# Moving the small convolution between two output products, and stores and scalings to other places, in a fused state-space scan kernel

## The chip, the core and the metric

The kernel runs on one core of a Trainium2 chip. The core has a matrix engine (TensorE, PE), a vector engine (VectorE, DVE), a scalar engine (ScalarE, ACT), a general engine (GpSimd, POOL) and a queue engine (SyncE, SP), from which nearly all transfers of this kernel are issued. The metric is the device time of one execution in microseconds.

## The reference

The input x is (4, 128, 96, 96) in float32. It is normalised in 32 groups of channels. Each image is then read as a sequence of 9216 positions in four directions: by rows forwards and backwards, by columns forwards and backwards. All four go through the same block, and its outputs are fused by a 1x1 convolution and added to x:

```python
t = grouped1x1(x, in_proj)            # 128 -> 512 channels, 4 groups
u, gate = t[:, :256], t[:, 256:]
u = depthwise_conv5(silu(u))
s = ssm_in @ u                        # 32 channels
a = clip(0.999 + 0.0009 * sigmoid(ssm_delta @ u + b), 0.0001, 0.9999)
bb, cc = tanh(ssm_b @ u + b), tanh(ssm_c @ u + b)
h = scan(h * a + bb * s)              # along the sequence (written with cumsums)
u = u + ssm_out @ (cc * h + d * s)
y = out_proj @ (grouped1x1(u * sigmoid(gate), mix))
```

## The kernel before, in words

Two directions are done together: as two streams s = 0 and 1, one forwards and one backwards. A *phase* is one image in one order (columns, V, or rows, H); there are eight. A phase has six *steps* of 1536 positions, a step four *pairs* of units (p = 0 to 3, one unit for each stream). A unit has 384 columns, every fourth position of the step. The main loop calls `pair(t)` for t = 0 to 191; k is t modulo 4. The work of several stages is overlapped by hand: in pair t

- the *front* (`front`, `compute_front`) computes silu of the input projection for pair t+4,
- the *convolution* and the *projections* (`taps`, `conv`, `conv_less`, `proj`) are done for pair t,
- the *scan* (`scan`) runs over half of the step before, when k is 0 or 1,
- `outputs` multiplies the state for pair t-5,
- the gates, `out_of` and `gating` finish pair t-6, whose product with the fused weights, W (`accumulate`), comes one pair later still.

The instruction order of every engine is the program's order, written out by hand.

Because the two streams run over one image from its two ends, in the second half of a phase they meet data that the first half has computed: silu is then loaded from a copy in DRAM (`keep_silu`, `load_silu`), and the gates too (`kept`, `load_kept`). So there are kinds of pairs. Counted by t modulo 24: in pairs 8 to 17 gates are computed and no front ("gates alone"); in 18 and 19 neither; in 20 to 23 and 0 to 5 a front, with gates loaded from DRAM (called `old`); in 6 and 7 both front and gates. The flag `ahead` is true in all but the first six pairs and pairs 6 and 7.

The 256 channels of u come in two halves. Half 0 is convolved on TensorE: `conv` (weights `band`, 128 rows by 32 columns of the array) and `conv_less` (weights `less`, 64 rows by 32 columns) add into two PSUM banks, and a copy for each stream brings the sum to `us[i]`. Half 1 is convolved by five taps: the first on ScalarE (`first_tap`, L609), four on VectorE (L611), with the running sum in PSUM banks 0 and 1. The same banks take the output products afterwards: `under` (L501) copies u there as the start of the sum, and `out_of` (L493) adds the matmuls of the state; the gating (L563) multiplies by the gate. Banks 4 to 7 are shared by W, convolution, gates and projections; in pairs without a front the convolution has banks 7 and 6, the two W have 4 and then 5, the projections 4 and 5, and the four gates the banks of `GATE[False]`.

In a gates-alone pair TensorE's order is: `conv`, W, W, `conv_less`, then four `gate` and four `out_of` matmuls (32 rows by 128 columns), then the projections. ScalarE's order is: first `under`, copy of W (L714 or L712), second `under`, copy of W, copies of u (L594; in pairs with k of 2 and 3 the second of them is VectorE's), four gate tanhs (L509), first tap, scaling of s (L664), and the three evacuations of the projections (L639 to L641). VectorE also takes bn_stats (L397) of the next image's chunks, in V phases with k of 2 and 3; the chunks are loaded by `load_chunks` (L393).

Of the kernel before, what the change touches and what calls it, by code (L numbers as in the profile page):

```python
# [55 lines left out]
R = 4  # L56
LN = 16
NS = HH // LN
N = LN * WW // R
# [7 lines left out]
def conv_preact_kernel(  # L67
# [51 lines left out]
    psum = ps.tile([P, 8, 512], F32, name="psum")  # L119
    SSM, TAPS, PROJ = 0, 0, (4, 5)  # L120
    FRONT = (7, 6, 2, 3)
    GATE = {True: (6, 4, 5, 7), False: (4, 5, 7, 6)}

    def plan(with_front):

# [2 lines left out]
    def bank(i):  # L128
        return psum[:, i, :]
# [287 lines left out]
    def front_parts(i, banks):  # L417

        step, g = divmod(i, R)
        if step * UB >= NU:  # L420
            return
        st = step % NS
        if st == NS // 2:
            sils[step] = sils[step - 1]
            load_silu(step + 1, (g,))
        elif st == NS - 1 and g < 2:
            load_silu(step, (2 * g, 2 * g + 1))
        elif g == 0 and fresh(step):
# [12 lines left out]
        for s in range(2):  # L441
            load_front(step + 1, s, slice(64 * s + 32, 64 * s + 64), slice(g, g + 1))
        if g == R - 1:
            for s in range(2):
                load_front(step + 1, s, slice(64 * s, 64 * s + 32), slice(0, R))
        if step:
            keep_silu(step, g)

    def keep_silu(step, g):
        st = step % NS  # L450
        if st < NS // 2 - 1:
            nc.sync.dma_start(kept_sil[step // NS % 2][st][g], sils[step][:, :, :, g, :])

    def load_silu(step, gs):
        if 0 in gs:
# [44 lines left out]
        seeded.add(bi)  # L500
        nc.scalar.copy(psum[:, SSM + 2 * s : SSM + 2 * s + 2, :N], us[bi][:, s])  # L501

    def sigmoids(bi, banks):
        bn = stats[units[bi]["b"]][1]
        n = bi // 2
        gv = gates[n % 2]
        for s in range(2):
            for j in range(2):
                nc.scalar.activation(  # L509
                    gv[:, s, j, :],  # L510
                    bank(banks[2 * s + j])[:, :N],
                    AF.Tanh,
                    bias=bn[:, 2 + j : 3 + j],
                    scale=0.5,
                )
# [49 lines left out]
    us = {}  # L565
# [10 lines left out]
    def conv(i, banks):  # L576

        step, p = units[i]["step"], units[i]["p"]
        sil, k = blocks(step), less_of(p)
        for s in range(2):  # L580
            for g in range(4):
                mm(bank(banks[s]), g, band[:, s, p, g, :], columns(step, sil[s][:, g, :], 1 - k),
                   True, False)

    def conv_less(i, banks, copies=(nc.scalar.copy, nc.scalar.copy)):
        step, p = units[i]["step"], units[i]["p"]
        sil, k = blocks(step), less_of(p)
        for g in range(4):
            for s in range(2):
                r = less_rows(s, p)  # L590
                mm(bank(banks[s]), g, less[r, p, g, :], columns(step, sil[s][r, g, :], k),
                   False, True)
        for s, copy in enumerate(copies):
            copy(us[i][:, s, 0, :], bank(banks[s])[:, :N])  # L594

    def new_u(i):
        us[i] = wk.tile([P, 2, 2, N], F32, tag="u", bufs=LAG + 2, name=f"u_{units[i]['id']}")
# [22 lines left out]
    scans, tbs, tms = {}, {}, {}  # L620
    qb, qc, qa, qs = (slice(MH * i, MH * (i + 1)) for i in range(4))

    def proj(i, banks):

        step, p = units[i]["step"], units[i]["p"]
        if step not in scans:
            t0 = wk.tile([P, N, R], F32, tag="t0", name=f"t0_{step}")
            scans[step] = t0.rearrange("p n r -> p r n")
        ta = scans[step]
        tb = tbs[i] = wk.tile([P, N], F32, tag="t1", bufs=LAG + 1, name=f"t1_{units[i]['id']}")  # L630

        for j in (1, 0):
            for bk, cols in zip(banks, ((qb, qb, qa, qa), (qs, qs, qc, qc))):
                for c in range(4):
                    mm(bank(bk), c, w_proj[:, j, cols[c]], us[i][:, c % 2, j, :], j == 1, j == 0)
        pa, pb = (bank(bk)[:, :N] for bk in banks)

        tm = tms[i] = wk.tile([P, N], F32, tag="tm", name=f"tm_{units[i]['id']}")
        nc.scalar.activation(tm, pa, AF.Tanh, bias=b_proj[:, 0:1])  # L639
# [93 lines left out]
        return add  # L733


    later = []

    waiting = []

# [7 lines left out]
    def pair(t):  # L747
        i, k, bi = 2 * t, t % R, 2 * (t - LAG)
        back = bi >= 0
        old = back and mirror(bi // 2) is not None  # L750

        late = bi > 2 and (bi - 2) % (NU // B) == 0
        with_front = fresh((t + R) // R)
        seed = old or back and not with_front

        ahead = old or back and not with_front
        banks, w = plan(with_front or not back)
        if back:
            front(t + R, FRONT)
        if seed and not with_front:  # L760
            under(bi, 1)
        send()

        if len(reload) == 4 and (k == 1 or late):
            for b, r in reload:
                nc.sync.dma_start(accf[:, r], xr[b, :, r])
            reload.clear()
        new_u(i)
        taps(i, range(1, K))
        if t and clip_late(i - 2):  # L770
            nc.vector.tensor_scalar(*decay(i - 2)[1])
        conv(i, banks)
        if not ahead:
            conv_less(i, banks)
        if not back:
            first_tap(i + 2)
            front(t + R, FRONT)
        recurrence(t)
        un = units[i]
        stats_chunks(t)  # L780

        def stats_piece():
            if later and k > 1:
                next(later[0], None)

        if not ahead:
            free[0] = w[1]
            stats_piece()
        if seed and with_front:
            for s in (1, 0):  # L790
                under(bi, s)
        if waiting and not late:
            accumulate(waiting.pop(0), w[0])()
        if seed and not with_front:
            under(bi, 0)
        if ahead:
            accumulate(waiting.pop(0), w[1])()
            free[0] = w[0]
            stats_piece()

            other = nc.vector.tensor_copy if k > 1 and not old else nc.scalar.copy
            conv_less(i, banks, (nc.scalar.copy, other))
        if old:
            for s in range(2):
                for j in range(2):
                    out_of(bi, s, j)
                load_gate(bi + s + UB)
        elif back:
            gates_and_out(bi, with_front)
        if back:  # L810
            for s in range(2):
                gating(bi, s)
        if un["order"] == "V" and un["b"] + 1 < B and un["st"] == NS - 1 and k == R - 1:
            later[:] = [stats_finish(un["b"] + 1)]
        if t + 1 < NU // 2:
            load_chunks(t + 1)
        if back:
            load_kept(bi // 2 + 2)
            if waiting:
                add = accumulate(waiting.pop(0), w[1])  # L820
                if not late:
                    add()
            first_tap(i + 2)
            scale_s(i - 2)
        if t == NU // 2 - 1:
            for s in range(2):
                under(bi + 2, s)
        proj(i, PROJ)
        if not back and t > 0:
            scale_s(i - 2)  # L830
        if late:
            add()
            accumulate(waiting.pop(0), w[1])()
        if back:
            waiting.extend(units[bi : bi + 2])
        if t == NU // 2 - 3:
            load_last()
        if t < R:
            keep_silu(0, t)

        if bi > 0 and bi % (NU // B) == 0:
            send()

    def tail():

        first, banks = NU // 2 - LAG, (6, 7, 4, 5)

        for op in decay(NU - 2):
            nc.vector.tensor_scalar(*op)
        scale_s(NU - 2)  # L850
# [127 lines left out]
```

## Time and profile before

| | |
|---|---|
| median time of 3 runs | 1869.56 us (1867.16 to 1872.62) |
| profiled run, span | 1866.4 us, mean granted clock 0.99 |
| TensorE busy | 1827.3 us, 98% |
| ScalarE, VectorE, GpSimd busy | 1542.6, 1561.9, 1567.0 us |
| share of SP's transfers in 16 DMA engines' time | 51.5% |
| mean traffic | 172 GB/s |

The profile page gives each engine's busy time, the clock, the chain of work that ended last, and groups of instructions by line. L133 is the helper that records most matmuls: they are told apart by the tiles they read (`w_fin` for W, `main` for the projections, `sil,band` and `sil,less` for the convolution). A float32 matmul stands as two passes in the trace.

### The profile page before, as it was taken

The page shows a single profiled execution, that of the slowest core. Times are in us where ns is not written, and L with a number is a line of the kernel's source. Part 1 is how long each engine was busy: PE and PEld are TensorE (multiplying, and loading weights), DVE is VectorE, ACT ScalarE, POOL GpSimd, SP SyncE. Part 2 cuts the span into 40 slices and gives each one's busy share as a digit, 9 for nine tenths or more (in the row PEclk, how much of TensorE's full clock was granted, in tenths as well). Part 3 has the DMA queues.
Part 4 walks back from the last instruction along what each step waited for, and adds up shares of the span by engine and source line. Part 5 has one row for each costly group of instructions (what it writes and reads, how often), then busy time and mean ns, then how long its engine had stood idle before and what let it go on. Part 6 is the DMA issues. An engine that isn't in the chain of part 4 may idle for free.

```text
span 1866.4 us, 57669 instructions
## 1 busy us (share of the span) xinstructions
PE 1827.3 (98%) x24024; PEld 691.4 (37%) x24024; DVE 1561.9 (84%) x1573; ACT 1542.6 (83%) x2841; POOL 1567.0 (84%) x1615
## 2 busy tenths in 40 slices
PE   6899999999999999999999999999999999999998
PEld 3234333443334433344333433334333443334432
DVE  4698878888888988888889898888887888878886
ACT  4688888888888888888888888888888888888875
POOL 6388988888879899888887989888888889997886
PEclk7999999999999999999999999999999999999999
DMA  5564463433875557243596556433467634535424
GB/s 194 162 197 145 146 207 118 168 141 126 274 244 202 169 155 215 86 158 131 186 301 217 167 162 207 152 130 126 139 224 234 231 113 156 191 118 175 145 102 171
DMA packets 147828, 321.21 MB, mean 172 GB/s; under 512 B 14192, under 2 KB 115696, under 8 KB 147568
## 3 DMA queue, kind: packets, MB, share of 16 engines
q1 hardware_dynamic: 147136, 316.56, 51.5%
q8 instruction: 190, 3.11, 0.7%
q10 hardware_dynamic: 432, 0.96, 0.1%
q14 instruction: 70, 0.57, 0.1%
HBM read 185.21 MB, written 132.25 MB: 170 GB/s over the span
## 4 chain that ended last, share of the span: by engine, by line
PE 87%; ACT 4%; POOL 3%; DVE 2%; DMA 1%; issue 1%; SPq 0%; POOLq 0%; DVEq 0%; ACTq 0%
PE psum L133 73%; PE psum L487 7%; PE psum L493 7%; ACT sil L476 1%; DMA xs<-in_xr 1%; ACT psum L609 1%; DVE u L563 1%; DVE psum L611 1%; POOL acc L728 1%; POOL t L644 1%; ACT u L594 0%; POOL t L647 0%; DMA x_in<-in_xs 0%; POOL t L687 0%; POOL t L688 0%
## 5 line engine op out<-in xcount | busy, mean ns | idle before, releaser
L611 DVE SCALAR_TENSOR_TENSOR psum<-sil,small,psum 128x768 f32<-128x768 f32 x576 | 589.0, 1023 | 39.1 <-ACT psum L609 13.5
L133 PE MATMUL psum<-u,w_fin 128*32 128x384 f32 x6144 | 535.6, 488 | 0.0
L133 PE MATMUL psum<-u,main 128*32 128x384 f32 x6144 | 534.9, 489 | 0.3 <-DVE u L611 0.3
L563 DVE SCALAR_TENSOR_TENSOR u<-gate,psum 128x768 f32<-128x768 f32 x376 | 349.9, 952 | 165.9 <-ACT u L594 91.6
L728 POOL TENSOR_TENSOR acc<-ys,acc 128x384 f32<-128x384 f32 x376 | 412.7, 1118 | 21.6 <-ACT ys L714 4.3
L687 POOL TENSOR_TENSOR t<-t,t 64x384 f32<-64x384 f32 x192 | 263.8, 1374 | 78.0 <-DVE t L681 58.0
L133 PEld LDWEIGHTS psum<-u,w_fin 128*32 128x32 f32 x6144 | 195.9, 110 | 303.3 <-issue 223.6
L501 ACT COPY psum<-u 128x768 f32<-128x768 f32 x352 | 277.6, 802 | 34.9 <-DVE u L611 28.8
L133 PE MATMUL psum<-sil,band 128*32 128x384 f32 x3072 | 291.9, 494 | 10.8 <-ACT tm L639 8.2
L133 PEld LDWEIGHTS psum<-u,main 128*32 128x32 f32 x6144 | 181.8, 109 | 324.9 <-issue 203.0
L644 POOL TENSOR_SCALAR t<-tm 64x384 f32<-64x384 f32 x191 | 177.9, 931 | 133.0 <-ACT tm L639 103.2
L688 POOL TENSOR_TENSOR t<-t,t 64x384 f32<-64x384 f32 x192 | 276.3, 1439 | 15.1
L609 ACT ACTIVATE psum<-sil,small 128x768 f32<-128x768 f32 x192 | 174.1, 907 | 104.6 <-DVE u L563 98.6
L493 PE MATMUL psum<-t,main 32*128 32x384 f32 x1536 | 240.2, 520 | 3.3 <-POOL t L688 1.5
L647 POOL TENSOR_TENSOR t<-t,tm 64x384 f32<-64x384 f32 x192 | 208.9, 1088 | 15.3
L509 ACT ACTIVATE gate<-psum,bnorm 128x384 f32<-128x384 f32 x384 | 194.8, 583 | 13.9 <-PE psum L487 7.7
L476 ACT ACTIVATE sil<-psum,bnorm 128x385 f32<-128x385 f32 x384 | 192.0, 585 | 11.7 <-DMA xs<-in_xr 5.4
L611 DVE SCALAR_TENSOR_TENSOR u<-sil,small,psum 128x768 f32<-128x768 f32 x192 | 194.9, 1015 | 7.8
L487 PE MATMUL psum<-x_in,wn 32*128 32x384 f32 x768 | 193.8, 521 | 0.5 <-ACT u L594 0.3
L594 ACT COPY u<-psum 128x384 f32<-128x384 f32 x352 | 153.1, 482 | 30.1 <-PE psum L133 21.8
L714 ACT COPY ys<-psum 128x384 f32<-128x384 f32 x287 | 132.5, 475 | 49.5 <-PE psum L133 41.5
L133 PE MATMUL psum<-sil,less 64*32 64x384 f32 x3072 | 168.8, 497 | 0.0
(87 smaller groups left out, 1642.0 us busy)
## 6 DMA issues: line engine op xcount, KB each, us to landing
sil<-sil SPq DMA_DIRECT2D x128, 770.0 KB, 6.2
kept<-gate SPq DMA_DIRECT2D x80, 768.0 KB, 3.9
gate<-kept SPq DMA_DIRECT2D x76, 768.0 KB, 5.0
x_in<-in_xs SPq DMA_DIRECT2D x192, 96.2 KB, 2.5
out<-acc SPq DMA_DIRECT2D x48, 384.0 KB, 6.1
acc<-in_xr SPq DMA_DIRECT2D x38, 384.0 KB, 6.3
xs<-in_xr SPq DMA_DIRECT2D x72, 192.0 KB, 5.1
x_in<-in_xs SPq DMA_DIRECT2D x184, 48.1 KB, 4.7
```

Of the source, the lines that this page charges most:

```text
L133: nc.tensor.matmul(o[r, : rhs.shape[-1]], lhsT, rhs, start=start, stop=stop, skip_group_check=True)
L476: nc.scalar.activation(sil[:, s, j, g, :], bank(banks[2 * s + j])[:, : N + 1], AF.Silu, bias=bn[:, 1:2] if j else bn[:, 4 + g : 5 + g],)
L487: nc.tensor.matmul(bank(to)[:, :N], stats[un["b"]][0][r, s, :], x_in[s][r, q, off : off + N], start=True, stop=True)
L493: nc.tensor.matmul(bank(SSM + 2 * s + j)[:, :N], w_so[r, bass.ts(j, P)], z[r, :], start=bi not in seeded, stop=True, skip_group_check=True)
L501: nc.scalar.copy(psum[:, SSM + 2 * s : SSM + 2 * s + 2, :N], us[bi][:, s])
L563: nc.vector.scalar_tensor_tensor(v, g, 1.0, pz, ALU.add, ALU.mult)
L611: nc.vector.scalar_tensor_tensor(us[i][:, :, 1, :] if k == K - 1 else part, src, w_tap[:, k : k + 1], part, ALU.mult, ALU.add,)
L644: nc.gpsimd.tensor_scalar(*op)
L647: nc.gpsimd.tensor_mul(ta[0:64, p, :], tb[0:64, :], tm[0:64, :])
L687: nc.gpsimd.tensor_mul(ta[0:64, p, :], tb[64:P, :], ta[64:P, p, :])
L688: nc.gpsimd.tensor_add(tb[0:64, :], ta[0:64, p, :], tb[0:64, :])
L728: adder.tensor_add(part, y, part)
```

## The change

The change has five parts.

1. In gates-alone pairs `conv_less` comes between the two W and not after them. The banks of the gates change from (4, 5, 7, 6) to (4, 7, 6, 5), and the tanhs of stream 1 are taken in the other order.
2. One copy on ScalarE brings u of both streams to SBUF, in all pairs. It needs the two banks in rising order, so the convolution's first bank is the lower one; VectorE takes no part any more.
3. In gates-alone pairs the projections finish bank 4 before bank 5 is begun, with half 0 first.
4. The scaling of s is moved: behind the projections' evacuations where gates are computed, and ahead of `out_of` in the mirrored pairs.
5. Silu's stores are gathered in a list, oldest first, and sent at the end of the pair, two in the first two pairs and then one. The loads of chunks and of kept gates are held until the next pair's front has issued its own loads.

It is meant to let TensorE go on while copies run, to take work from VectorE, and to give urgent loads the way.

```diff
-    GATE = {True: (6, 4, 5, 7), False: (4, 5, 7, 6)}
+    GATE = {True: (6, 4, 5, 7), False: (4, 7, 6, 5)}
...
-        if step:
-            keep_silu(step, g)
-
-    def keep_silu(step, g):
-        st = step % NS
         if st < NS // 2 - 1:
-            nc.sync.dma_start(kept_sil[step // NS % 2][st][g], sils[step][:, :, :, g, :])
+            to_keep.append((step, g))
+
+    to_keep = []
+
+    def keep_silu(n):
+        for step, g in to_keep[:n]:
+            nc.sync.dma_start(kept_sil[step // NS % 2][step % NS][g], sils[step][:, :, :, g, :])
+        del to_keep[:n]
...
-            for j in range(2):
+
+            for j in (0, 1) if s == 0 or to[0] == GATE[True][0] else (1, 0):
...
-        sil, k = blocks(step), less_of(p)
+        sil, k, b0 = blocks(step), less_of(p), min(banks)
...
-        for s, copy in enumerate(copies):
-            copy(us[i][:, s, 0, :], bank(banks[s])[:, :N])
+        nc.scalar.copy(us[i][:, :, 0, :], psum[:, b0 : b0 + 2, :N])
...
-    def proj(i, banks):
+    def proj(i, banks, apart=False):
...
-        for j in (1, 0):
-            for bk, cols in zip(banks, ((qb, qb, qa, qa), (qs, qs, qc, qc))):
-                for c in range(4):
-                    mm(bank(bk), c, w_proj[:, j, cols[c]], us[i][:, c % 2, j, :], j == 1, j == 0)
+        turns = [(e, j) for j in (1, 0) for e in range(2)]
+        for e, j in sorted(turns) if apart else turns:
+            for c, cols in enumerate(((qb, qb, qa, qa), (qs, qs, qc, qc))[e]):
+                first, end = (j == 0, j == 1) if apart else (j == 1, j == 0)
+                mm(bank(banks[e]), c, w_proj[:, j, cols], us[i][:, c % 2, j, :], first, end)
...
             front(t + R, FRONT)
+
+        for load in soon:
+            load()
+        soon.clear()
...
+
+        if ahead and not old:
+            conv_less(i, banks)
         if ahead:
             accumulate(waiting.pop(0), w[1])()
+            if old:
+                conv_less(i, banks)
             free[0] = w[0]
             stats_piece()
-
-            other = nc.vector.tensor_copy if k > 1 and not old else nc.scalar.copy
-            conv_less(i, banks, (nc.scalar.copy, other))
         if old:
+            scale_s(i - 2)
...
         if t + 1 < NU // 2:
-            load_chunks(t + 1)
+            soon.append(lambda: load_chunks(t + 1))
         if back:
-            load_kept(bi // 2 + 2)
+            soon.append(lambda: load_kept(bi // 2 + 2))
...
-            scale_s(i - 2)
...
-        proj(i, PROJ)
-        if not back and t > 0:
+        proj(i, PROJ, ahead and not old)
+        if not old and t > 0:
             scale_s(i - 2)
...
-        if t < R:
-            keep_silu(0, t)
+        keep_silu(2 if t < 2 else 1)
```

More of the change, by code (lines that the diff above doesn't have):

```diff
@@ L501, in under, with sigmoids @@
         nc.scalar.copy(psum[:, SSM + 2 * s : SSM + 2 * s + 2, :N], us[bi][:, s])
-    def sigmoids(bi, banks):
+    def sigmoids(bi, to):
         bn = stats[units[bi]["b"]][1]
@@ L507, in sigmoids @@
         for s in range(2):
-            for j in range(2):
+            for j in (0, 1) if s == 0 or to[0] == GATE[True][0] else (1, 0):
                 nc.scalar.activation(
                     gv[:, s, j, :],
-                    bank(banks[2 * s + j])[:, :N],
+                    bank(to[2 * s + j])[:, :N],
                     AF.Tanh,
@@ L578, in conv, with conv_less @@
         step, p = units[i]["step"], units[i]["p"]
-        sil, k = blocks(step), less_of(p)
+        sil, k, b0 = blocks(step), less_of(p), min(banks)
         for s in range(2):
             for g in range(4):
-                mm(bank(banks[s]), g, band[:, s, p, g, :], columns(step, sil[s][:, g, :], 1 - k),
+                mm(bank(b0 + s), g, band[:, s, p, g, :], columns(step, sil[s][:, g, :], 1 - k),
                    True, False)
-    def conv_less(i, banks, copies=(nc.scalar.copy, nc.scalar.copy)):
+    def conv_less(i, banks):
         step, p = units[i]["step"], units[i]["p"]
-        sil, k = blocks(step), less_of(p)
+        sil, k, b0 = blocks(step), less_of(p), min(banks)
         for g in range(4):
@@ L590, in conv_less @@
                 r = less_rows(s, p)
-                mm(bank(banks[s]), g, less[r, p, g, :], columns(step, sil[s][r, g, :], k),
+                mm(bank(b0 + s), g, less[r, p, g, :], columns(step, sil[s][r, g, :], k),
                    False, True)
-        for s, copy in enumerate(copies):
-            copy(us[i][:, s, 0, :], bank(banks[s])[:, :N])
+        nc.scalar.copy(us[i][:, :, 0, :], psum[:, b0 : b0 + 2, :N])
     def new_u(i):
@@ L733, in accumulate @@
         return add
-    later = []
+    later, soon = [], []
     waiting = []
@@ L846, in tail @@
         first, banks = NU // 2 - LAG, (6, 7, 4, 5)
+        for load in soon:
+            load()
         for op in decay(NU - 2):
```

## The prediction

> **What bounds the kernel now.** I read the page first (busy shares, chain, DMA queue), then the waits, then the timeline of single pairs (a pair is one turn of the main loop, two units; I cut it from the start of its projections to the next start), and last the two places where a pair takes far longer than its like.
>
> From the page:
>
> ```profile
> PE 1827.3 (98%) x24024; PEld 691.4 (37%) x24024; DVE 1561.9 (84%) x1573; ACT 1542.6 (83%) x2841; POOL 1567.0 (84%) x1615
> ...
> PE 87%; ACT 4%; POOL 3%; DVE 2%; DMA 1%; issue 1%; SPq 0%; POOLq 0%; DVEq 0%; ACTq 0%
> ```
>
> TensorE carries the chain. But a matmul that waits behind another still looks busy, so the shares don't show how full a pair is. From the timeline of a pair with gates and no front (start 642.12, the next 651.42, so 9.30 us):
>
> ```profile
> 642.12 2.79 PE L133 MATMUL psum<-u,main 128*32 128x384 f32 x32
> 642.24 1.90 DVE L563 SCALAR_TENSOR_TENSOR u<-gate,psum 128x768 f32<-128x768 f32 x2 [0.21 <-ACT gate L509]
> ...
> 643.23 0.91 ACT L609 ACTIVATE psum<-sil,small 128x768 f32<-128x768 f32 x1
> ...
> 647.35 1.01 DVE L611 SCALAR_TENSOR_TENSOR u<-sil,small,psum 128x768 f32<-128x768 f32 x1
> ...
> 648.39 0.80 ACT L501 COPY psum<-u 128x768 f32<-128x768 f32 x1 [0.30 <-DVE u L611]
> ...
> 648.71 0.88 PE L133 MATMUL psum<-sil,less 64*32 64x384 f32 x16
> 649.13 0.47 ACT L714 COPY ys<-psum 128x384 f32<-128x384 f32 x1
> ...
> 649.51 0.73 PE L487 MATMUL psum<-x_in,wn 32*128 32x384 f32 x2
> ...
> 649.67 0.86 ACT L594 COPY u<-psum 128x384 f32<-128x384 f32 x2
> ...
> 650.46 1.53 ACT L509 ACTIVATE gate<-psum,bnorm 128x384 f32<-128x384 f32 x3
> ```
>
> See here a loop through three engines. The gating (DVE L563) frees the PSUM banks of the taps, the first tap (ACT L609) fills them, four taps end at 648.36, `under` (L501) copies, then ACT stores W (L714), both u copies (L594) and the gate tanhs (L509), after which the next gating starts. Call P the start of the projections and g the start of the gating. Two stretches repeat: from P to the next g 9.426 us (gate matmuls start at P+7.393, first tanh 0.945 later, 0.479 to the second, 0.576 for it, 0.033 hand-over), and from g to the P after it 9.185 (6.122 to the end of the taps, 2.173 to the end of the second u copy, 0.052, then 0.427+0.411 for the last gate matmul and the return to projections). Half their sum is 9.305, the pair's time. So gates-alone pairs are set by this crossed loop, not by TensorE, whose own work would allow about 8.9.
>
> Pairs of the mirrored half take 8.25 (no front) or 9.26 (front), with no wait on TensorE; pairs six and seven of each 24 take about 10.2.
>
> Two stalls stand apart. At the start:
>
> ```profile
> 63.81 1.25 SPq L452 DMA_DIRECT2D sil<-sil  x2
> ...
> 74.75 2.00 ACT L476 ACTIVATE sil<-psum,bnorm 128x385 f32<-128x385 f32 x4 [5.36 <-DMA xs<-in_xr]
> ...
> 77.27 2.79 PE L133 MATMUL psum<-sil,band 128*32 128x384 f32 x16 [5.18 <-ACT tm L639]
> ```
>
> The named load is not what silu needs: it overwrites the buffer of step 0, whose last store (the second L452, issued 64.44; the longest landing of L452 is 10.1) is read out until then. That pair takes 13.41 where the ones before it take 6.9 to 7.1. And at the first pair of the second pass:
>
> ```profile
> 253.78 0.88 PE L133 MATMUL psum<-x_in,wn 32*32 32x385 f32 x16 [0.25 <-DMA x_in<-in_xs]
> ...
> 255.52 0.88 PE L133 MATMUL psum<-x_in,wn 32*32 32x385 f32 x16 [0.87 <-DMA x_in<-in_xs]
> ```
>
> These loads were issued at 246.3 and 247.0, behind two chunk loads and a 768 KB gate load: 12.96 us for a pair of 9.3.
>
> **What the Trainium skill says.** TensorEngine Tiling (Array Packing), Key Properties: a change of tiling mode drains TensorE. The trace agrees: passes start every 0.322 us, but 0.435 apart where 128-row turns to 64-row, 0.46 where 64-row ends, and the first pass after a change takes 0.347. PSUM — Partial Sum Buffer, PSUM bank collisions: two engines may not use one bank's quadrant at once, so a matmul waits for the copy out of its bank; the trace has it (second gate matmul 0.055 after the W copy ends). TensorE: Matmul & The Clock Gate, Part 1: after an idle window the clock is halved; here passes after both stalls take 0.62 to 0.64. DMA: Bandwidth & Descriptors, Queues, rings and completion order: each DMA engine takes descriptors in ring order, so a load stands behind an earlier store; the 8.4 us of those x loads agree.
>
> **The change, part by part.**
>
> *Small conv between both W, u in one copy, gates in banks 4, 7, 6, 5 (80 pairs).* TensorE leaves and re-enters the 128-row mode once more: 0.113+0.025 = 0.14 us. So the gate stage starts at P+7.53. The first gate (bank 4) is free at once; first tanh 7.53+0.945 = 8.475, second 8.954, next g at P+9.563 (was 9.426). The second gate now lies in bank 7 and waits for the u copy. ACT takes work in order: W copy, `under` (waits for the taps), u copy, second W copy. From the end of the taps: 0.835 to the end of `under`, then one copy of 128x768. No such copy is in the trace; the bounds are 0.80 (L501, same size, other way) and 0.86 (both halves). I take 0.80, less 0.06 overlap: ends at 1.575. The second gate matmul is the head of TensorE's queue, so the four output matmuls and the two gates behind it wait too: start 1.63, its passes and those behind it 0.427+0.325+0.322, return 0.411, so g to P is 6.122+1.63+1.485 = 9.237. The third and fourth tanh come later as well and delay gating and taps by about 0.06. Half the sum: (9.563+9.237+0.06)/2 = 9.43; without the 0.06, 9.40. Against before: 40 ordinary pairs at 9.316: +0.1 each, +4. 8 first pairs after a front stretch, 10.11: the wait for the longer ACT chain, +0.2, +1.6. 32 pairs that had a half copied by DVE: mean 9.415, because bn_stats often held that DVE copy back (10.0 beside 9.05); now 9.42, and three with statistics matmuls still about +1: +3. In sum +8.5.
>
> *Projections bank by bank, s scaled later.* The tanh of bank 4 can start earlier, but the first tap holds ACT until P+2.0 in any case; hidden in gates-alone pairs. In front pairs with the mirrored half, the scaling (0.60) leaves the place before that tanh, which then starts 0.38 earlier (2.15, when bank 4 is done). Where conv waited for it (pairs of 9.33 instead of 9.26, some 24), -0.07 each: -1.7. Moved behind the u copy, the scaling sits in ACT's idle second before the next first tap: nothing.
>
> *One u copy in pairs six and seven.* The third gate waited for the end of both copies, 6.875; now 6.81: -0.06 for 16, -1.
>
> *Silu stores.* Step 0's four stores now go out in pairs 0 and 1, not 0 to 3: done by about 54 by my estimate (four times 770 KB from 41 us on), long before silu of step 2 (70.1). The stall and the half clock after it go: 13.41 to 7.1, -6.3. The x load before it (8.37 for a pair of 7.1) has one store less ahead: -1.2.
>
> *Chunk and kept-gate loads after the x loads.* At 246 the x loads then have 1.15 MB less in front, at 270 GB/s 4 us: the stall of 3.65 goes, I take -3.3. The price: the chunk loads in pairs with x loads wait in SP's queue for the front matmuls and are issued some 3 to 5 us later (about P+5 to 6.5); bn_stats is wanted at P+7.3 to 8.3. At their shortest landing, 2.5, they are just in time, at 5.1 up to 3 us late. What is behind bn_stats on DVE is the gating; it has 0.7 us of slack there. About ten such pairs: from 0 to +20; I take +1. Kept gates have 18 us from issue to use: nothing.
>
> Sum: 8.5 - 1.7 - 1 - 7.5 - 3.3 + 1 = -4.0; 1869.6 - 4.0 = 1865.5.
>
> **The rivals.**
> 1. *TensorE sets the gates-alone pairs.* If the u copy is out before the gates begin, a pair is the drain-free stage 8.88 + 0.14 + 0.1 for the first tanh leaving bank 4 = 9.12. 72 pairs of it and 8 of 9.9: 736 where they took 755; with the other savings of 12.5, 1838. For it: the copy no longer comes after the second W. Against it: `under`, which waits for DVE, stands before it on ACT.
> 2. *Slower: late chunks and a longer ACT chain.* Gates-alone pairs at 9.5 (+15), chunk waits +10, savings 12.5: 1882. For it: DMA moves 250 to 290 GB/s in those stretches; against it: the slack of 0.7.
> 3. *The stalls only move*, since the same bytes must pass: the start and pair 24 give nothing, 1876. Against it: the DMA engines are idle at 80 to 90 us (2 GB/s).
>
> **How the numbers follow.** Forecast 0.42, rivals 0.20, 0.23, 0.15. Range: 1838 to 1884, from the first rival to just over the second. Faster than 1864: the first rival and over half of the forecast, 0.45. Within 0.3% (1864 to 1875): the rest of the forecast and part of the third, 0.22. Slower: 0.33.
>
> **What would show it.** Right: gates-alone pairs at 9.40 to 9.43; the second L487 matmul starting 0.05 after the L594 copy of 128x768; no idle before silu near 70 us, and passes of 0.32 throughout the start; no wait for x_in near 250 us. Wrong: gates-alone pairs near 9.1 or over 9.5, DVE waiting for xs by more than the 6.6 us of now, or the stall near 74 us still there.

## The result, and the profile after

The changed kernel takes 1898.63 us (median of 4 runs, 1893.27 to 1901.24), beside 1871.09 us for the kernel before on the same chip (the three runs above and one more). The ratio is 1.0147 (95% interval 1.0118 to 1.0175): 27.5 us slower, where 4.0 us less was forecast.

The two lines of the page after that answer to those of before, busy time and chain:

```profile
PE 1846.4 (97%) x24024; PEld 665.9 (35%) x24024; DVE 1539.7 (81%) x1541; ACT 1561.9 (82%) x2681; POOL 1560.9 (82%) x1615
...
PE 83%; ACT 6%; DVE 4%; DMA 3%; POOL 1%; issue 1%; SPq 1%; DVEq 0%; ACTq 0%; POOLq 0%
```

TensorE's share of the chain falls from 87% to 83%; ACT, DVE and DMA each gain two points. So something on these three now ends the waits. In the list of waits of the kernel after, one line with a DMA in it has grown:

```profile
DVE bn L397 <- DMA xs<-in_xr: 44.2, 25, 5.5
```

(in order: us in all, times, longest). Before it was 6.6 us, 4 times.

To see where the time goes I cut both traces into pairs, as in the prediction (pair t ends where the projections of pair t start), and added the lengths by kind of pair. The numbers in the last three columns come from experiments below; the table is worked out from the traces of single executions, whose spans (1866.4 and 1899.5) lie 33 us apart where the medians lie 27.5 apart. "Mirrored" are the pairs with gates loaded from DRAM; all but four of them have a front.

| kind of pair (t modulo 24), number | before | after | e1_chunks_early | n1_best_parts | s1_conv_upper_first |
|---|---|---|---|---|---|
| pairs 1 to 7 of the start, 7 | 63.0 | 61.4 | 54.2 | 54.4 | 54.5 |
| first gates-alone pair (8), 8 | 80.9 | 86.4 | 85.1 | 83.9 | 83.5 |
| gates alone (9 to 17), 72 | 673.9 | 684.0 | 682.5 | 669.2 | 669.2 |
| neither (18, 19), 16 | 132.0 | 132.0 | 132.0 | 132.0 | 132.0 |
| mirrored (20 to 23, 1, 2, 5), 53 | 491.1 | 496.3 | 496.3 | 489.2 | 489.1 |
| mirrored (3, 4, 0), 21 | 202.2 | 213.9 | 201.7 | 197.5 | 197.8 |
| gates and front (6, 7), 14 | 143.3 | 144.2 | 144.2 | 144.2 | 144.2 |

Of the 33 us between the two traces, 17 lie in the mirrored pairs, 10 in the 72 gates-alone pairs and 5.5 in the eight pairs 8.

**Gates-alone pairs are as forecast.** The timeline of one, after, from 640.84 to 650.27:

```profile
640.84 2.79 PE L133 MATMUL psum<-u,main 128*32 128x384 f32 x32
640.97 0.95 DVE L566 SCALAR_TENSOR_TENSOR u<-gate,psum 128x768 f32<-128x768 f32 x1 [0.61 <-PE psum L489]
...
646.14 0.88 PE L133 MATMUL psum<-sil,less 64*32 64x384 f32 x16
...
647.93 0.79 ACT L596 COPY u<-psum 128x768 f32<-128x768 f32 x1
...
648.37 0.99 PE L489 MATMUL psum<-x_in,wn 32*128 32x384 f32 x2
...
649.32 1.72 ACT L512 ACTIVATE gate<-psum,bnorm 128x384 f32<-128x384 f32 x3 [0.21 <-PE psum L489]
...
650.27 0.53 PE L133 MATMUL psum<-u,main 128*32 128x384 f32 x4
650.40 0.95 DVE L566 SCALAR_TENSOR_TENSOR u<-gate,psum 128x768 f32<-128x768 f32 x1 [0.93 <-PE psum L489]
```

Read it against the forecast, with P = 640.84: gates start at P+7.53 (forecast 7.53), the first tanh at P+8.48 (8.475), the next gating at P+9.56 (9.563). The u copy of 128x768 takes 0.797 (0.80 was taken), and the second gate (the other instruction of the 648.37 row) starts at 648.78, 0.05 after that copy ends. The pair is 9.43 long.

**A mirrored pair with a front is not.** The same stretch of one, before:

```profile
694.12 0.88 PE L133 MATMUL psum<-sil,less 64*32 64x384 f32 x16
...
694.92 0.93 PE L493 MATMUL psum<-t,main 32*128 32x384 f32 x8
695.08 0.86 ACT L594 COPY u<-psum 128x384 f32<-128x384 f32 x2
...
695.78 0.16 PEld L133 LDWEIGHTS psum<-u,main 128*32 128x32 f32 x8 [0.55 <-ACT u L594]
695.78 0.85 PE L133 MATMUL psum<-u,main 128*32 128x384 f32 x8
```

and after:

```profile
693.30 0.88 PE L133 MATMUL psum<-sil,less 64*32 64x384 f32 x16
...
694.11 0.93 PE L495 MATMUL psum<-t,main 32*128 32x384 f32 x8
694.29 0.80 ACT L596 COPY u<-psum 128x768 f32<-128x768 f32 x1 [0.28 <-PE psum L133]
...
695.14 0.16 PEld L133 LDWEIGHTS psum<-u,main 128*32 128x32 f32 x8 [0.72 <-ACT u L596]
695.14 0.85 PE L133 MATMUL psum<-u,main 128*32 128x384 f32 x7
```

(The last row counts 7 passes where the one before counts 8, since this view ends at 695.5.) From `conv_less` to the projections it takes 1.66 before and 1.84 after. In pairs with a front the convolution has banks 4 and 5, and these are the banks of the projections. Before, the first of the two copies (0.48) was out at 695.56, so bank 4, in which the projections begin, was free when TensorE came to them at 695.78; the second copy ended only at 695.94, beside their first passes. Now one instruction reads both banks, its end at 695.09 is the only event that frees either, and TensorE stands until 0.05 after it. The Trainium skill, PSUM — Partial Sum Buffer, PSUM bank collisions, has the rule that semaphores guard access bank by bank (and quadrant by quadrant); a copy over two banks guards both by one event, and the trace has the price: 9.26 becomes 9.44, and 9.33 becomes 9.50. There are 70 such pairs: at 0.17 each, 12 us. The table's sums show less than this, since some pairs that were late before, 9.8 to 13 us long, are shorter in the change.

**The start.** Timeline after, at pair 3, where the silu stall of before is gone:

```profile
59.15 0.56 DVE L397 BATCH_NORM_STATS2 bn<-xs 128x6 f32<-128x384 f32 x1 [5.46 <-DMA xs<-in_xr]
...
61.53 0.56 DVE L397 BATCH_NORM_STATS2 bn<-xs 128x6 f32<-128x384 f32 x1 [1.82 <-DMA xs<-in_xr]
62.01 3.12 DVE L613 SCALAR_TENSOR_TENSOR psum<-sil,small,psum 128x768 f32<-128x768 f32 x3
...
66.33 5.35 PE L133 MATMUL psum<-u,main 128*32 128x384 f32 x32 [4.79 <-DVE u L613]
...
76.15 1.05 ACT L478 ACTIVATE sil<-psum,bnorm 128x385 f32<-128x385 f32 x2
```

No idle stands ahead of silu (L478) any more, but bn_stats on DVE waits for chunks, the taps behind it come late, TensorE is idle for 4.79 us, and its next 32 passes take 5.35 and not 2.79 us (the Trainium skill, TensorE: Matmul & The Clock Gate, Part 1: the clock is halved after an idle window; the trace agrees, with a granted clock of 0.50 from 66.4 to 71.4). The pair takes 11.50.

**Late chunks in the passes.** The queue of SP in the pair from 704.57 to 714.01, after, by its own timeline:

```profile
708.29 2.99 SPq L252 DMA_DIRECT2D x_in<-in_xs  x4
711.38 1.01 SPq L393 DMA_DIRECT2D xs<-in_xr  x2
712.48 0.38 SPq L529 DMA_DIRECT2D gate<-kept  x1
```

and what DVE does with it:

```profile
714.32 0.56 DVE L397 BATCH_NORM_STATS2 bn<-xs 128x6 f32<-128x384 f32 x1 [2.79 <-DMA xs<-in_xr]
...
716.35 0.56 DVE L397 BATCH_NORM_STATS2 bn<-xs 128x6 f32<-128x384 f32 x1 [1.46 <-DMA xs<-in_xr]
...
716.82 1.80 DVE L566 SCALAR_TENSOR_TENSOR u<-gate,psum 128x768 f32<-128x768 f32 x2
```

The x loads wait for the front's matmuls; the chunk loads stand behind them and go out at 711.4. DVE is ready for bn_stats at 711.5, gets it at 714.3, and the gating, which is next on DVE and frees the banks of the taps, starts at 716.8. The next pair is 11.40 long instead of 9.33.

### The profile page after: what moved, and what is told of

Same layout as the page of the kernel before. It is cut to its first block, busy times and chain, and to the rows that moved or that the text cites. A ratio compares the mean times of both kernels' runs of the same rounds, so it can differ in the third digit from the quotient of the medians.

```text
span 1899.5 us, 57421 instructions
## 1 busy us (share of the span) xinstructions
PE 1846.4 (97%) x24024; PEld 665.9 (35%) x24024; DVE 1539.7 (81%) x1541; ACT 1561.9 (82%) x2681; POOL 1560.9 (82%) x1615
## 4 chain that ended last, share of the span: by engine, by line
PE 83%; ACT 6%; DVE 4%; DMA 3%; POOL 1%; issue 1%; SPq 1%; DVEq 0%; ACTq 0%; POOLq 0%
PE psum L133 72%; PE psum L495 5%; PE psum L489 5%; ACT u L596 3%; DMA xs<-in_xr 2%; DVE psum L613 2%; DVE u L566 1%; ACT sil L478 1%; ACT psum L611 1%; DMA gate<-kept 0%; DVE u L613 0%; ACT ys L717 0%; SPq L252 0%; POOL t L647 0%; POOL t L690 0%
## 5 line engine op out<-in xcount | busy, mean ns | idle before, releaser
L133 PE MATMUL psum<-u,w_fin 128*32 128x384 f32 x6144 | 553.2, 490 | 0.0
L133 PEld LDWEIGHTS psum<-u,w_fin 128*32 128x32 f32 x6144 | 188.1, 110 | 322.6 <-issue 218.7
L691 POOL TENSOR_TENSOR t<-t,t 64x384 f32<-64x384 f32 x192 | 287.6, 1498 | 15.1
L512 ACT ACTIVATE gate<-psum,bnorm 128x384 f32<-128x384 f32 x384 | 201.7, 578 | 30.9 <-PE psum L489 14.4
L650 POOL TENSOR_TENSOR t<-t,tm 64x384 f32<-64x384 f32 x192 | 203.9, 1062 | 15.3
L478 ACT ACTIVATE sil<-psum,bnorm 128x385 f32<-128x385 f32 x384 | 191.5, 584 | 5.4 <-POOL band L343 3.3
L596 ACT COPY u<-psum 128x768 f32<-128x768 f32 x192 | 153.0, 797 | 26.4 <-PE psum L133 25.7
```

Source lines behind the costliest of these rows:

```text
L133: nc.tensor.matmul(o[r, : rhs.shape[-1]], lhsT, rhs, start=start, stop=stop, skip_group_check=True)
L478: nc.scalar.activation(sil[:, s, j, g, :], bank(banks[2 * s + j])[:, : N + 1], AF.Silu, bias=bn[:, 1:2] if j else bn[:, 4 + g : 5 + g],)
L596: nc.scalar.copy(us[i][:, :, 0, :], psum[:, b0 : b0 + 2, :N])
L691: nc.gpsimd.tensor_add(tb[0:64, :], ta[0:64, p, :], tb[0:64, :])
```

## The experiments

The theory from the two traces: two things cost more than was forecast, the held chunk loads and the one copy in mirrored pairs; the gates-alone part costs about what was forecast. The rival: it is the gates-alone part and the longer ScalarE chain altogether, and the waits for chunks are a symptom of it.

**Chunks early.** The changed kernel, with the chunk loads issued where they were before.

```diff
-            soon.append(lambda: load_chunks(t + 1))
+            load_chunks(t + 1)
```

> The chunk loads are issued at the end of the pair before again; all else as in the changed kernel. Theory (late chunks hold up bn_stats, and the gating and taps behind it on VectorE): the 44 us that VectorE waited for xs fall under 10, the third pair of the start falls from 11.5 to about 7.1, pairs 3, 4 and 0 of each 24 fall to 9.44; 15 to 20 us less than the changed kernel, 1879 to 1884. Rival (the same bytes must pass, another transfer is late instead): 1892 to 1899, with waits for x_in in place of xs.

1878.82 us (1878.46 to 1880.52), ratio to before 1.005 (1.0035 to 1.0065): 19.8 us less than the change. DVE waits 2.2 us for chunks. The start takes 54.2 where it took 61.4, mirrored pairs 3, 4 and 0 201.7 where they took 213.9; nothing else moves by more than 1.5. Pair 24, 12.96 before and 10.94 after, is now 9.50. So the held chunk loads cost about 20 us, and among that is most of what the stores had gained and what pair 24 was to gain.

**Two copies.** The changed kernel, with the copy of u in two halves, both on ScalarE.

```diff
-        nc.scalar.copy(us[i][:, :, 0, :], psum[:, b0 : b0 + 2, :N])
+        for s in range(2):
+            nc.scalar.copy(us[i][:, s, 0, :], bank(b0 + s)[:, :N])
```

> u is copied for each stream by itself again, both on ScalarE; all else as in the changed kernel. Theory (in mirrored pairs with a front the convolution's banks are the projections' banks, so these wait for the end of the one copy, 0.17 us later than for its first half): those pairs fall from 9.44 to 9.26, gates-alone pairs stay at 9.43 within 0.05; about 13 us less, 1884 to 1887. Rival (the moved scaling of s delays ScalarE there): they stay at 9.44, 1896 to 1900.

1895.04 us (1888.31 to 1898.03), ratio 1.014 (1.012 to 1.0161). The mirrored pairs with a front are back at 9.26: the one copy is their cause, and the scaling, which is still at its new place, is not. Gates-alone pairs rise from 9.43 to 9.49, since the two halves take 0.86 on the chain and the one copy 0.80. In the trace the mirrored pairs gain 16 us, the gates-alone pairs lose 4 of it, and the span is 1886.6; about 6 of the 16 come from pairs in which the chunks happened to be less late. The median lies only 3.6 under the change, with runs from 1888 to 1898, and misses the 1884 to 1887 that were expected. So the run is read by its pairs, and its time shows no gain clear of noise.

**Gates-alone part undone.** The changed kernel with the small convolution after both W again, gates in banks 4, 5, 7, 6, tanhs in rising order, and projections in the old order.

```diff
-    GATE = {True: (6, 4, 5, 7), False: (4, 7, 6, 5)}
+    GATE = {True: (6, 4, 5, 7), False: (4, 5, 7, 6)}
...
-        if ahead and not old:
-            conv_less(i, banks)
         if ahead:
             accumulate(waiting.pop(0), w[1])()
-            if old:
-                conv_less(i, banks)
             free[0] = w[0]
             stats_piece()
+            conv_less(i, banks)
...
-        proj(i, PROJ, ahead and not old)
+        proj(i, PROJ)
```

> The small convolution stands after both W again, the banks and tanh order of the gates and the order in the projections are as in the kernel before; one copy of u, stores, loads and scalings as in the changed kernel. Theory (crossed loop through TensorE, ScalarE and VectorE): gates-alone pairs fall from 9.43 to 9.28 to 9.31, 10 to 14 us less, 1885 to 1889. Rival (the one copy on ScalarE makes them slow, not its place): they stay over 9.4.

1883.34 us (1881.26 to 1885.64), ratio 1.0073 (1.0054 to 1.0091). Gates-alone pairs are 9.27 in the median, shorter than before (9.30; those where DVE copied a half 9.42 in the mean): 671.0 for the 72, where the change has 684.0. So the gates-alone part costs 13 us beside the same kernel without it. The run takes back the place of the small convolution, the banks of the gates, and the order of tanhs and projections together, and doesn't tell them apart. Before did not show all of this, since the 72 pairs there, with copies on DVE, were 3 longer than here. Mirrored pairs stay at 9.44 and DVE still waits 40.0 us for chunks: the rival falls as the account of these two, which don't come from the gates-alone part. But that part is no small one: this run is 15.3 us under the change.

**Stores alone.** The kernel before, with the list of silu stores and nothing else.

```diff
-        if step:
-            keep_silu(step, g)
...
         if st < NS // 2 - 1:
...
+            to_keep.append((step, g))
...
-        if t < R:
-            keep_silu(0, t)
+        keep_silu(2 if t < 2 else 1)
```

> The kernel before with the list of silu stores alone. Theory (the stall at 74 us is the overwriting of step 0's silu while its last store still reads it): the 13.4 us pair falls to about 7.1, 5 to 8 us less than before, 1863 to 1866. Rival (the stall moves to another load): within 2 us of before.

1866.85 us (1863.69 to 1870.03), ratio 0.998 (0.9974 to 0.9987). The start falls by 8.5 (7.5 was forecast), so the stall's cause is shown. The time falls by less than the 5 to 8 us that were expected: mirrored pairs 3, 4 and 0 rise by 6.5: the weight loads of TensorE wait 12.1 us for x_in, 3.8 before. The stores now go out just ahead of x loads, at pairs' ends. In the kernels where the kept-gate loads are held too (e1 and n1) there is no such wait; so the list seems to need the held kept gates, though no run took these two apart.

**What holds, together.** From these: the changed kernel with its gates-alone part undone, chunks early, and the one copy everywhere but in mirrored pairs with a front.

```diff
...
-        nc.scalar.copy(us[i][:, :, 0, :], psum[:, b0 : b0 + 2, :N])
+        if b0 == PROJ[0] and i >= 2 * LAG and mirror(i // 2 - LAG) is not None:
+            for s in range(2):
+                nc.scalar.copy(us[i][:, s, 0, :], bank(b0 + s)[:, :N])
+        else:
+            nc.scalar.copy(us[i][:, :, 0, :], psum[:, b0 : b0 + 2, :N])
...
```

> The parts that paid: silu stores in the list, kept gates held until after the x loads, chunk loads early, the gates-alone order of the kernel before with one copy of u on ScalarE, but two copies in mirrored pairs with a front, where the projections take the same banks. If the three causes are separate and add up: gates-alone pairs 9.27, mirrored pairs with a front 9.26, the start 9 us shorter, 1850 to 1857, faster than both kernels. If the causes share a limit: over 1862.

1853.38 us (1852.96 to 1853.91), ratio 0.9918 (0.9903 to 0.9932): faster than both kernels. Mirrored pairs 9.26, gates-alone 9.27, start 54.4, DVE's wait for chunks 2.4.

**One copy alone.** The kernel before, with the one copy on ScalarE in all pairs.

> The kernel before with one copy of u on ScalarE in all pairs, nothing else. Theory: mirrored pairs with a front go from 9.26 to 9.44 (some 70 of them, +12), gates-alone pairs to 9.27 (-7): 1873 to 1878. Rival (the moved scaling makes the mirrored pairs slow): they stay at 9.26, 1862 to 1866.

1872.26 us (1870.52 to 1874.96), ratio 1.0014 (1.0005 to 1.0024). Mirrored pairs with a front 9.44 and gates-alone pairs 9.27, from before's own code: the copy's loss and its gain (-4.7 in the 72 gates-alone pairs, where DVE copies no more) are both shown alone. Of the 70 mirrored pairs with a front, 58 are longer by about 0.17, 10 us in all; the 70 together are 6.6 longer, since some late pairs of before are shorter here. One of these is pair 24: it takes 9.50 and TensorE waits for no x load in it, though the loads stand where before has them. So the stall of 12.96 there can end without the change's order of loads. Pair 7, in three phases, is 9.64 (9.68 before). Pair 8 is 11.3 to 12.5 in the same phases (10.7 to 10.8 before), which is taken up below.

**The u copy ahead of the second `under`.** The changed kernel, gates-alone pairs, with ScalarE's copy of u before it waits for the taps.

```diff
+        if ahead and not old:
+            conv_less(i, banks)
         if seed and not with_front:
             under(bi, 0)
-
-        if ahead and not old:
-            conv_less(i, banks)
```

> The changed kernel, with the small convolution and the copy of u ahead of the second under in gates-alone pairs, so that the copy doesn't stand behind VectorE's taps on ScalarE. Theory (crossed loop): the second gate starts on time, under ends at P+7.8, the outputs behind it wait for that, and a pair takes about 9.31; 80 pairs, 8 to 12 us less than the changed kernel. Rival (the extra change of tiling mode is all of the loss): 9.43 as before.

1881.68 us (1880.9 to 1887.01), ratio 1.0067 (1.0051 to 1.0084). Its timeline in a gates-alone pair:

```profile
648.87 0.80 ACT L596 COPY u<-psum 128x768 f32<-128x768 f32 x1 [0.31 <-PE psum L133]
...
649.57 0.81 ACT L503 COPY psum<-u 128x768 f32<-128x768 f32 x1
...
650.12 0.59 PE L489 MATMUL psum<-x_in,wn 32*128 32x384 f32 x2
...
650.31 0.48 ACT L717 COPY ys<-psum 128x384 f32<-128x384 f32 x1
...
651.07 2.05 ACT L512 ACTIVATE gate<-psum,bnorm 128x384 f32<-128x384 f32 x4 [0.27 <-PE psum L495]
```

The copy is out 0.45 before the gates begin, so bank 7 no longer holds them, and the pair falls from 9.43 to 9.32. That is still over the 9.27 without the move: the gates still begin 7.53 behind P, where they begin at 7.39 in e3_gates_part_undone, and half of these 0.14 is about what is left. So the crossed loop of the prediction is supported from a second side, and of the 0.16 that the gates-alone part costs a pair, `under` ahead of the copy makes 0.11.

**Chunks ahead of the x loads.** The changed kernel, with the held loads sent before the front, not after it.

```diff
-        if back:
-            front(t + R, FRONT)
-
         for load in soon:
             load()
         soon.clear()
+        if back:
+            front(t + R, FRONT)
```

> The changed kernel, with the held loads issued ahead of the front of the next pair and not after it. If SP stands at the x loads, which wait for TensorE's front matmuls, and the chunks behind them are late for that: waits for xs fall from 44 us to under 10 and the time to about 1880, as with chunks issued early. If the silu store, which still stands ahead of them, is what holds them back: waits over 25 us, and 1890 or more.

1886.32 us (1883.38 to 1887.68), ratio 1.0092 (1.0077 to 1.0107). DVE's wait for chunks falls from 44.2 to 8.9 and mirrored pairs 3, 4 and 0 to 201.8, as with early chunks: in the passes it is the standing of SP at the x loads that makes chunks late, not the half pair of delay. What is left to e1 is mostly the start, 58.7 to its 54.2, where the held chunks go out behind the pair's silu stores; so the time lies between the two that were expected, 1880 and 1890.

**Pair 8.** The first gates-alone pair of each 24 grew from 10.78 to 11.6 to 12.5 in three phases, and from 9.70 to 9.96 in the others (n1_best_parts: 11.79 and 9.69). The pair before it is the one in which both W of the last unit come late (`late`). Two causes offered themselves: with rising banks the convolution begins in bank 6, which that W still holds until it is copied to ys; and the scaling, now behind the evacuations, stands ahead of that copy on ScalarE. Four runs, two of them n1_best_parts with one edit, one with both, and the scaling's move alone on the kernel before:

```diff
-        for s in range(2):
+        for s in (1, 0) if b0 == 6 else (0, 1):
             for g in range(4):
...
```

> n1_best_parts with one thing more: where the convolution has banks 6 and 7, its matmuls begin in bank 7 (the stream order 1, 0), as they did before. It asks what makes pair 8 of each 24 long (before 10.78 in three phases and 9.70 in the others; after 11.6 to 12.5 and 9.96; n1_best_parts 11.79 and 9.69). Theory 'bank': pair 8 follows the pair whose W come last, the W in bank 6 is copied out late, and the convolution now begins in that bank; then pair 8 falls from 11.79 to about 11.0, some 3 us over the whole, 1850.5. Rival 'scaling': the scaling of s, moved behind the evacuations, holds that copy of W back on ScalarE, and the order of the banks hardly matters; then pair 8 stays within 0.2 of 11.79 and the time at 1853.

> n1_best_parts with the scaling of s at the places it had before (ahead of the projections' evacuations in all pairs with a back end). Theory 'bank': pair 8 keeps most of its length, about 11.4, which n2_one_copy_alone had with one copy and the scaling unmoved. Rival 'scaling': it falls to 10.8. Apart from this, pair 7, which is 10.12 in three phases wherever the scaling was moved (after, e1, e2, e3, n1) and 9.64 to 9.68 where it wasn't (before, e4, n2), should fall to 9.65 if the moved scaling is its cause, 1.4 us over the whole, and stay at 10.12 if it isn't. Time: 1851 with both small gains, 1853.4 with none; if the scaling's move had a gain of its own in the mirrored pairs, those would go from 9.26 to more.

> The kernel before, with the scaling of s moved to the places of the change, and nothing else. If the moved scaling costs pair 7: 9.68 becomes 10.15 there in three phases. Pair 8: theory 'bank' leaves it within 0.3 of 10.78, since the convolution still begins in bank 7; rival 'scaling' lengthens it to 11.5 or more. My prediction had a gain of 0.07 in the mirrored front pairs of 9.33 (the scaling leaves the place ahead of the tanh of the projections): 9.33 becomes 9.26 if that holds, stays if not. In sum 1870 to 1873, of which a difference to before of +1.4 would be the pairs 7.

> n1_best_parts with both: the convolution begins in bank 7, and the scaling stands where it was before. Theory 'bank': pair 8 at about 10.8 and pair 7 at 9.65, 1849 us. If the two effects don't add (the copy of W waits for something else), pair 8 stays over 11.3 and the time is 1851 or more.

Phases are counted from 0.

| | median us | ratio to before | pair 8, phases 2, 4, 6 | pair 8, others | pair 7, phases 2, 4, 6 |
|---|---|---|---|---|---|
| before | 1870.53 | 1 | 10.78, 10.80, 10.73 | 9.70 | 9.68 |
| s1 (bank 7 first) | 1851.54 | 0.9893 (0.9876 to 0.991) | 11.93, 11.92, 11.14 | 9.70 | 10.12 |
| s2 (scaling back) | 1857.06 | 0.992 (0.9902 to 0.9938) | 11.38, 11.37, 11.34 | 9.64 | 9.64 |
| s3 (scaling alone) | 1866.90 | 0.9978 (0.9971 to 0.9985) | 11.18, 12.14, 11.18 | 9.80 | 10.17 |
| s4 (both) | 1855.40 | 0.9913 (0.9896 to 0.9929) | 10.76, 12.28, 10.69 | 9.64 | 9.64 |

Both theories hold in part, and add: beginning in bank 6 costs 0.6 (11.34 to 10.7, s2 to s4), the scaling 0.4 (10.78 to 11.18, before to s3), together the 1.0 of n1_best_parts. But where pair 8 was to fall, it did so only in some phases, and the times of s2 (1851 to 1853.4 expected) and s3 (1870 to 1873) missed what was expected; s4 is not at the 1849 of theory 'bank', in part since its pairs 1 are longer again (see below). The pairs of about 12 have another cause; the timeline of s1, phase 2:

```profile
548.07 0.85 PE L133 MATMUL psum<-sil,band 128*32 128x384 f32 x8 [0.40 <-ACT ys L721]
...
548.96 3.83 POOL L735 TENSOR_TENSOR acc<-ys,acc 128x384 f32<-128x384 f32 x2
...
549.97 1.82 DVE L688 TENSOR_TENSOR_SCAN t<-t,t 64x768 f32<-64x768 f32 x1
...
552.82 0.48 ACT L721 COPY ys<-psum 128x384 f32<-128x384 f32 x1 [1.28 <-POOL acc L735]
...
553.20 0.80 ACT L600 COPY u<-psum 128x768 f32<-128x768 f32 x1
```

The next copy of W needs a ys buffer that GpSimd's add still reads. Two adds take 2.4 elsewhere, 3.83 here, because the second met DVE's scan (last section). It ends at 552.79, and the copies of ys and u wait for it. A stretched add of 2.6 to 2.7 stands in all six pairs 8 of about 12 us of s1, s3, s4, n2 and e1, and in no other pair 8 of these runs. The change's own 12.51 and 12.40 (phases 2 and 4) are not of this kind: their adds take 1.22 at most, and bn_stats waits 1.6 and 1.5 for a chunk in the pair before. Phase 6, whose image has no successor and so no chunks, has 11.63.

The scaling's move shows gains as well: s3 is faster than before by 0.2%, and s1 than s4, which differ in the scaling alone, by 3.9 us in the median, 2.8 in the profiled runs. In pair 1 of every second phase, where the gating comes late, the scaling stood between the first tap and the evacuations; these four pairs take 9.5 to 9.6 with it moved (s1) and 10.4 to 10.5 with it back (s4), 3.4 us in sum. The gain lies there, not in the pairs of 9.33, which stay.

s1_conv_upper_first is the fastest kernel here, though its interval overlaps that of n1_best_parts. From its page, busy time and chain:

```profile
PE 1817.8 (98%) x24024; PEld 693.4 (37%) x24024; DVE 1546.0 (84%) x1541; ACT 1585.7 (86%) x2751; POOL 1565.5 (85%) x1615
...
PE 91%; ACT 4%; POOL 3%; issue 0%; DVE 0%; POOLq 0%; DVEq 0%; ACTq 0%
```

TensorE's share of the chain is 91%, four points over before, and DMA is no longer in it.

## Why the prediction was wrong

The forecast was -4.0 and the measurement is +27.5, outside the range and beyond every rival. Two sums of the prediction are off by 0.1 (4 + 1.6 + 3 is 8.6, 1869.6 - 4.0 is 1865.6), which changes nothing. By the prediction's own steps:

- *What bounds the kernel, and the crossed loop:* right. Gates-alone pairs were to be 9.40 to 9.43 and are 9.43, event by event; n3 moved one of the loop's terms and got 9.32, where 9.31 was expected. The first rival (TensorE sets these pairs, 9.12) is refuted.
- *Small conv between both W, u in one copy:* right for the 72 ordinary pairs (+7 forecast, +8.6 with chunks early, +10.1 in the change), too small for the first pairs after a front (+1.6 forecast; +4.2 and +5.5). In five of these eight pairs the +0.2 each was about right (+0.22 to +0.27), and it goes when the gates-alone part is undone (9.69). In the three others, phases 2, 4 and 6, it is +0.9 to +1.7, and the cause I gave, a longer ScalarE chain, is not the one: it is bank 6 first and the scaling before ys, and on top of them late chunks or late ys buffers. The change of the convolution's first bank was costed nowhere.
- *The same step, mirrored pairs:* **this is a step that failed.** I costed the one copy in gates-alone pairs and in pairs six and seven, and at nothing in the mirrored pairs with a front. The question I did not ask is which instruction writes next into each bank that the merged copy reads: here it is the projections, and the first of them had started on a half. It costs 0.17 in each of 70 pairs, 10 to 12 us; the 0.17 is shown by e2 (the copy split) and n2 (the copy alone).
- *Projections bank by bank, s scaled later (-1.7):* the pairs of 9.33 stay at 9.33 when only the scaling moves (s3). A gain came elsewhere, in four late pairs (3.4 between s4 and s1), and pair 7 and pair 8 pay for part of it. That the move gains at all is luck: the mechanism is not the one forecast.
- *One u copy in pairs six and seven (-1):* -0.04 in three pairs (n2), about what was worked out for each, but the move of the scaling adds 0.48 there (9.64 beside 10.12, s4 and s1): +1 in sum.
- *Silu stores (-7.5):* right, -8.5 alone in e4. In the change only -1.7 is left of it, because the chunks are late in the same stretch.
- *Chunk and kept-gate loads after the x loads:* the number of the gain was right (-3.3 forecast at pair 24, -3.5 with chunks early), but its cause is not shown, as n2 has the same 9.50 with the loads unmoved. **The price was the larger mistake, and the other step that failed**: +1 taken, out of a bound of 0 to +20, and it is about 20 (e1). The issue was forecast at P+5 to 6.5; in the pair shown the two chunks went out at P+6.8 and 7.4. I gave the gating 0.7 us behind bn_stats and took the shortest landing, 2.5; these two took 2.9 and 4.3, both came late, and the next pair took 11.40. I also left the start out of this step: there the chunks go out behind the silu stores, the first two landed 8.0 and 9.0 after their issue, and bn_stats waited 5.46 and 1.82 for them.

The second rival (slower, 1882) named two of the places, the gates-alone pairs (+15) and the chunks (+10, half of what they cost), and had no mirrored pairs. The third (stalls only move) holds for the stores in the change, but not by itself: with early chunks the stalls vanish. It was the named sign "DVE waiting for xs by more than the 6.6 us" that told at once.

Left open: the stretched add as the cause of pairs 8 of about 12 us is read from traces, and I made no run that took it away. No run moves the x loads alone, so it is open what ends the stall at pair 24. Nor does one tell the parts of the gates-alone change apart, beyond n3.

## What to carry to other kernels

When two evacuations are merged into one instruction, list for each PSUM bank who writes it next: the first bank now comes free at the end of the whole copy, and a saving of 0.06 on one path was a loss of 0.17 on another, in about as many pairs.

A load held back to let another pass is only as early as the wait in front of that other. Ask where the issuing queue itself stands still, not only how much slack the data has, and look at what is queued behind the consumer: here bn_stats carried the gating, and the gating the next pair.

A change of several parts is best tried part by part. By the runs and the sums of pairs, this one held some 20 us of gain (stores 8.5, pair 24 3.5, moved scaling 3.4, one copy in gates-alone pairs 4.7) under some 48 of loss (chunks 20, the gates-alone part 13, one copy in mirrored pairs 12, pair 8 3). The parts kept, with the convolution beginning in bank 7 again, give 0.9893 of the time before.

## What the runs showed of the hardware

A GpSimd add (64x384) and DVE's scan (`t<-t,t`, 64x768) get in each other's way. In the trace after, all 36 of the adds of L691 that start within a scan take 2.50 to 2.57 us and end 0.97 to 1.04 after the scan does; the 155 that don't meet a scan take 1.22 in the median. Scans that start inside a GpSimd instruction take 2.27 in the median (69), the others 1.82 (27). The Trainium skill says this: SBUF — State Buffer, Who interferes with whom, has a VectorE instruction with two SBUF inputs and a GpSimd instruction that reads SBUF exclude each other through a shared port, held for the whole instruction. The trace agrees in direction and in order. The prediction had not counted it, and it fits the pairs 8 of about 12 us that have a stretched add. It was read from traces, not tried by a run of its own.

A ScalarE copy of 128x768 out of two banks takes 0.797 us, two of 128x384 take 0.48 each and 0.86 together.
